# Step sizes of a Mamba-2 mixer with weights loaded instead of tokens, packed in column groups of the array

## The chip, the cores and the metric

The kernel runs on one core of a Trainium2 chip. The metric is the time of one execution on the device in microseconds (us). The median of three runs of the kernel before is 1029.48 us (1029.3 to 1030.61). All data are 32-bit floats, apart from the packed weights of the feed-forward part.

The names of the engines in the profile: PE is TensorE (matmuls), PEld its weight loads, DVE is VectorE, ACT is ScalarE, POOL is GpSimd, SP is SyncE, which here only issues DMAs.

## The reference

The input is 4 sequences of 1024 tokens with 256 features. One layer is applied: `x + norm(mixer(norm(x)))`, then `x + norm(ffn(norm(x)))`. What matters here, cut to its core:

```
zxbcdt = u @ in_proj_kernel            # [.., 256] @ [256, 1288]
z, xBC, dt = 512, 768 and 8 columns of it
xBC = silu(causal_conv1d(xBC))         # x (512), B (128), C (128)
dt  = softplus(dt + dt_bias)           # the step sizes: one per token and head, 8 heads
dA  = dt * -exp(A_log)                 # running sums of dA give all decays of the scan
... chunked state scan with these decays, gate with silu(z), norm, output projection
ffn: gate and up [2048, 256] and down [256, 2048], unpacked from 4-bit codes; gelu(gate) * up
```

The change touches the eight columns of the projection that give `dt`.

## The kernel before

**Segments.** The tokens are cut into nine segments: two of 256 tokens (segments 0 and 1) and seven of 512 (2 to 8). Each goes through a mixer (`mixer(s)`) and a feed-forward part (`ffn(s)`). A segment is worked in chunks of 128 tokens: NC is 2 in the short ones and 4 in the long ones.

**Recorder and planner.** No instruction is issued where it is written. A `Recorder` writes down each one as a step with the tiles that it reads and writes; `issue` then plans all steps on a clock of its own (costs in `weigh`, in ns) and emits them in the planned order. Each engine executes its own list strictly in that order and waits on semaphores. At each moment the planner takes, for an engine, the step with the lowest `rank` among those that could start within a short patience (150 ns in the beginning, 30 ns later); ties go to the earlier recorded. A step's `floor` is the earliest time that the planner may give it. Because all steps go through one helper, every instruction of the profile carries line L347; the tiles' names tell them apart.

**Ranks.** `mix` steps of segment s+2 rank ahead of the matmuls of `ffn(s)`. So the mixer two segments ahead goes first wherever its inputs are there, and the feed-forward matmuls fill the rest of TensorE's time.

**Tiles.** Two PSUM banks of pool `a` serve the mixers from segment 2 on (`ps_a()` hands them out), four of pool `f` and two of pool `d` the feed-forward part. In segment 0 the mixer uses pool `f`, in segment 1 `a` and `d` in turn. A bank is given out in the order in which it was asked for; a later request may pass an earlier one only where two banks are free (`may_start`):

```
if at >= self.ahead or at >= len(self.waiting) or (at > 0 and len(self.free) < 2):
    return None
```

**The mixer's front.** `norm_in` normalises the tokens, turns each chunk with TensorE and copies the result to `xnT`, in two halves of 128 features (kk = 0, 1), each [128 features x 512 tokens]. `step_sizes` multiplies these with the last eight columns of `win` (the projection's weights). In it the tokens are the loaded operand: for each chunk and half, a 128x128 block of `xnT` is loaded and eight columns of `win` are streamed through; the result lies with tokens on partitions. In the profile these matmuls are the group `a<-win,xnT` (and `f<-` and `d<-` in segments 0 and 1). Then VectorE adds the bias (`dtv<-a,dtb`), and a chain of small VectorE operations with one exponential on ScalarE (`dte<-dte`) gives `dt` and `da`. Later `features(f)` makes the 768 columns of xBC (`a<-xnT,win`, four passes of 256 or 512 streamed columns each for a pair of halves), with the convolution on VectorE, and `decays` makes the running sums of `da` (`a<-upper,da`, `a<-da,upper` and so on).

A 32-bit matmul is two rows in the profile: two weight loads and two passes of the moving operand. A transpose is one.

**Feed-forward.** From segment 2 on, each product uses seven sub-products with precomputed weight blocks. These lie in DRAM (`stock`), and `fetch(k)` loads block k (1.8 MB) to one of two halves of `wide`. The first two fetches of segment 2 overwrite the plain gate and up weights, which segments 0 and 1 read; they stand in SP's queue (`wide<-stock`) with the mixer's loads `e<-rows`, `r<-rows`, the input loads `x<-in_u_dram` and the output stores `out_dram<-fo`.

Of the kernel before, what the change touches and what calls it, by code (L numbers as in the profile page):

```python
# [13 lines left out]
ALU = mybir.AluOpType  # L14
PSUM = bass.MemoryType.PSUM

P = 128
EPS = 1e-5
NB, L, DM = 4, 1024, 256
DI, NH, HD, DS = 512, 8, 64, 128  # L20
DPROJ = 2 * DI + 2 * DS + NH
# [9 lines left out]
SWITCH = 1400.0  # L31
WARM, WARM_FROM = 40, 9000.0
EARLY = 150000.0
FRONT = 2 + 1 + NF
MASKED = -1.0e30
MLP = 2048
# [110 lines left out]
class Recorder:  # L147
# [78 lines left out]
    @staticmethod  # L226
    def weigh(st):

        e, n = st.engine, st.n
        if e == "PE":  # L230
            cols = Recorder.width(st.shapes[0])
            if st.name == "transpose":
                return max(109.0, cols * 0.42), 220.0
            if st.shapes[0][0] == 64:
                return 109.0, 220.0
            return 140.0 if cols == 1 else 2 * max(100.0 if cols < 64 else 109.0, cols * 0.837), 220.0
        if e == "DVE":
            if st.name == "bn_stats":
                return 60 + n * 1.05, 130.0
            if st.name == "tensor_scalar" and bass.MemoryType.PSUM not in st.space:  # L240
                return 70 + n * 0.53, 130.0
            return 65 + n * 1.05 + (0 if st.name == "tensor_tensor" else 20), 130.0
        if e == "ACT":
            st.table = {AF.Exp: "exp", AF.Gelu_apprx_tanh: "gelu"}.get(
                st.args[2] if len(st.args) > 2 else None)
            if st.name == "dma_start":
                return 500.0, 0.0
            acc = 93 if "accum_out" in st.kwargs else 0
            return 110 + n * 0.72 + 75 * st.pointers + acc, 160.0
        if e == "POOL":  # L250
            if st.name == "memset":
                return 60 + n * 1.2, 70.0
            if ALU.pow in st.args:
                return 523.0, 70.0
            if st.name == "affine_select":
                return 40 + n * 1.0, 70.0
            return (250 if n < 40 else 60 + n * 1.9), 70.0
        return 60.0, 0.0

    def issue(self, tc, rank, patience):  # L260


# [16 lines left out]
        while len(order) < len(steps):  # L279
# [29 lines left out]
            if e == "ACT" and st.table:  # L309
                table = st.table  # L310
            turn = min(PORT, max(0.0, free["POOL"] - t)) if st.port and t < EARLY else 0.0
            free[e] = t + st.busy + turn
# [50 lines left out]
def rank(st):  # L363
    kind, s = st.key
    if kind == "ffn":
        return 25 + 10 * s if st.engine == "PE" else 5
    if kind == "down":
        return 27 + 10 * s
    return {"load": 0, "small": 11, "mix": 10 + 10 * s if s < 2 else max(21, 10 * s - 10), "w": 14 + 10 * s, "z": 13, "const": 12,
            "warm": 1000, "wu": 11, "x": 5}[kind]  # L370


# [1 line left out]
def mamba_ffn_kernel(  # L374
# [19 lines left out]
    r = Recorder(tc.nc)  # L394
# [4 lines left out]
    def pool(name, shape, k=1, ahead=2, of=None, dtype=F32):  # L399
        of = of or sb  # L400
        return Pool([of.tile(shape, dtype, name=f"{name}{j}") for j in range(k)], ahead)

    def fixed(name, shape):
        return pool(name, shape).get()

    def given(ap):
        return Pool([ap]).get()

    u, w_in, conv_w, conv_b, dt_bias, a_log, d_skip, norm_w, w_out = map(
        given, (u, w_in, conv_w, conv_b, dt_bias, a_log, d_skip, norm_w, w_out))  # L410
    g_pack, g_scale, u_pack, u_scale, d_pack, d_scale, out = map(
        given, (g_pack, g_scale, u_pack, u_scale, d_pack, d_scale, out))
# [5 lines left out]
        "x": pool("x", [P, CMAX, DM], 3), "xnT": pool("xnT", [P, 2, TMAX]),  # L418
        "xc": pool("xc", [P, NF, TMAX]), "xn": pool("xn", [P, DM], 2, 3), "th": pool("th", [P, TMAX], 3, 3),
        "sz": pool("sz", [P, DI // P, TMAX]), "r": pool("r", [P, DI // P, P], 2), "e": pool("e", [P, NH, P], 2),  # L420
        "bt": pool("bt", [P, DS], 2), "xdt": pool("xdt", [P, NH, HD], 2),
        "xw": pool("xw", [P, NH, HD], 2), "y": pool("y", [P, DI // P, P], 3),
        "yo": pool("yo", [P, DI // P, P]), "xf": pool("xf", [P, 2, P], 2),
        "xfT": pool("xfT", [P, 2, TMAX], 2), "act": pool("act", [P, HALF], 3, 3),
# [10 lines left out]
    def get(tag):  # L435
        return pools[tag].get()


    def rows_of(s):
        b, t0, T = SEGS[s]  # L440
        return b * L + t0, T
# [3 lines left out]
    def by_segment(s, tag, cut):  # L445

        if s > 1:
            return cut(get(tag), slice(0, SEGS[s][2]))
        if tag not in shared:
            shared[tag] = get(tag)  # L450
        return cut(shared[tag], slice(SEGS[s][1], SEGS[s][1] + SEGS[s][2]))
# [3 lines left out]
    def load_x(s):  # L455
        r0, T = rows_of(s)
        x = by_segment(s, "x", lambda t, c: t[:, c.start // P : c.stop // P, :])
        r.floor = (0.0, 0.0, 40000.0)[min(s, 2)]
        r.sync.dma_start(out=x, in_=u[r0 : r0 + T, :].rearrange("(i p) d -> p i d", p=P))
        r.floor = 0.0  # L460
        xs[s] = x

    win = fixed("win", [P, 2, DPROJ])

    def load_win(c0, c1, queue=r.sync):
        queue.dma_start(out=win[:, :, c0:c1],
                         in_=w_in[:, c0:c1].rearrange("(k p) m -> p k m", p=P))

    r.key = ("load", 0)
    load_x(0)  # L470
    load_win(2 * DI, DPROJ)
    load_win(DI, 2 * DI)
    small_loads = {}
# [10 lines left out]
    dtb, aneg, cw, cb, dsk, nw = [small_loads[k] for k in ("dtb", "aneg", "cw", "cb", "dsk", "nw")]  # L484
# [3 lines left out]
    ident = fixed("ident", [P, P])  # L488
# [48 lines left out]
    def little(tag, n):  # L537
        return get(tag)[:, :n]
# [118 lines left out]
    def mixer(s):  # L657
# [3 lines left out]
        NC = T // P  # L661
        W = NC * NH
        v_ = {}

        def ps_a():

            v_["n"] = v_.get("n", 0) + 1
            if s == 0:
                return banks_f.get()
            return (banks_d if s == 1 and v_["n"] % 2 else banks_a).get()  # L670
# [17 lines left out]
        def step_sizes():  # L688

            xnT = v_["xnT"]  # L690
            pdt = ps_a()
            for i in range(NC):
                for kk in range(2):
                    r.tensor.matmul(pdt[:, i * NH : (i + 1) * NH],
                                     lhsT=xnT[:, kk, i * P : (i + 1) * P],
                                     rhs=win[:, kk, DPROJ - NH : DPROJ],
                                     start=(kk == 0), stop=(kk == 1))
            v = little("dtv", W)
            r.vector.tensor_tensor(v.rearrange("p (i h) -> p i h", h=NH),
                                    pdt[:, :W].rearrange("p (i h) -> p i h", h=NH),  # L700
                                    dtb.unsqueeze(1).to_broadcast([P, NC, NH]), ALU.add)
            e = little("dte", W)
            r.vector.scalar_tensor_tensor(e, v, -1.0, v, ALU.mult, ALU.max)
            r.scalar.activation(e, e, AF.Exp, scale=-1.0)

            z = little("dtz", W)
            r.vector.tensor_scalar(z, e, 2.0, None, ALU.add)
            r.vector.reciprocal(z, z)
            r.vector.tensor_tensor(z, z, e, ALU.mult)
            z2 = little("dtz2", W)  # L710
            r.vector.tensor_tensor(z2, z, z, ALU.mult)
            r.vector.tensor_scalar(e, z2, 1.0 / 17.0, None, ALU.mult)
            for k in (15, 13, 11, 9, 7, 5, 3):
                r.vector.scalar_tensor_tensor(e, e, 1.0 / k, z2, ALU.add, ALU.mult)
            r.vector.scalar_tensor_tensor(e, e, 1.0, z, ALU.add, ALU.mult)
            r.vector.tensor_scalar(e, e, 2.0, None, ALU.mult)
            dt = v_["dt"] = little("dt", W)
            r.vector.scalar_tensor_tensor(dt, v, 0.0, e, ALU.max, ALU.add)
            da = v_["da"] = little("da", W)
            r.vector.tensor_tensor(da.rearrange("p (i h) -> p i h", h=NH),  # L720
                                    dt.rearrange("p (i h) -> p i h", h=NH),
                                    aneg.unsqueeze(1).to_broadcast([P, NC, NH]), ALU.mult)
# [237 lines left out]
        for j in range(NC + 4):  # L960
            for d, stage in enumerate((inner, scan, gated, way_out, turned)):
                i = j - d
                if 0 <= i < NC:
                    steps.append(lambda stage=stage, i=i: stage(i))
                if d == 0 and j < 2:
                    steps += [lambda c=c: gate(c) for c in (2 * j, 2 * j + 1)]
        assert len(steps) == FRONT + 5 * NC + DI // P
        return steps


    def ffn(s):
        b, t0, T = SEGS[s]
        r0, _ = rows_of(s)
        NC = T // P
# [28 lines left out]
            r.vector.tensor_tensor(at[:, n, :], a, bank[:, T : 2 * T], ALU.mult)  # L1003

        def fetch(k):
            r.sync.dma_start(out=blocks[k % 2], in_=stock[k])

        def token_sums():
            x = xfT[s]
# [93 lines left out]
    mix = [mixer(s) for s in range(ns)]  # L1103

    def do(kind, s, steps):
        for step in steps:
            r.key = (kind, s)
            step()
# [6 lines left out]
    for k in range(WARM):  # L1115
        r.floor = WARM_FROM + k * 220.0
        r.tensor.matmul(idle[:, k % 4 * P : (k % 4 + 1) * P], lhsT=ident, rhs=ident,
                        start=(k == 0), stop=True, skip_group_check=True)
    r.floor = 0.0
    do("mix", 0, mix[0][:FRONT])  # L1120

# [8 lines left out]
    r.floor = 0.0  # L1130
    do("mix", 0, mix[0][FRONT:])
    do("mix", 1, mix[1][:FRONT])
    do("mix", 1, mix[1][FRONT:])
    for s in range(ns):
# [67 lines left out]
```

## Time and profile before

| | us |
|---|---|
| median of three runs | 1029.48 |
| the profiled execution | 1027.49 |
| its span in the profile | 1025.8 |
| PE busy | 1006.5 |
| DVE busy | 637.2 |
| ACT busy | 505.4 |
| matmuls of step sizes, all nine segments (x128) | 16.0 |

The page's busy times are sums over one execution. Matmul rows overlap: a row's length is the latency of one pass, and the distance between the starts of successive rows is what a pass costs TensorE in a stream. The 16.0 us in the last line are the busy time of the three groups (13.2, 1.7 and 1.1 us).

### The profile page before, as it was taken

To read this page: it belongs to the slowest core of one execution; us is meant where nothing else is said; L and a number is where in the kernel's file an instruction comes from. 1 tells how busy PE (TensorE), PEld (TensorE's weight loads), DVE (VectorE), ACT (ScalarE), POOL (GpSimd) and SP (SyncE) were. 2 spreads that over 40 slices of the span, in tenths; PEclk is the share of its full clock that TensorE was granted. 3 is DMA by queue.
4 is the path that set the end of the run, shared out by engine and by line. 5 is a ranking of instruction groups with operands and counts; after the bars stand their busy time and mean duration, and the time that the engine had idled before them with its cause. 6 is when DMAs were issued, how large, how long until landed. Compare 5 with 4: busy or idle time off the path is not lost.

```text
span 1025.8 us, 14550 instructions
## 1 busy us (share of the span) xinstructions
PE 1006.5 (98%) x5174; PEld 808.3 (79%) x5174; DVE 637.2 (62%) x1387; ACT 505.4 (49%) x1224; POOL 291.7 (28%) x475
## 2 busy tenths in 40 slices
PE   7999999989999999999999999999999999999997
PEld 6789877867788668877887778877887788888886
DVE  4896775557665766667676757586568674332431
ACT  4645845427472476336655636466446653332330
POOL 1726643430232113403340235003520145001001
PEclk8999999999999999999999999999999999999999
DMA  7032331414132223113312322231323230242300
GB/s 254 10 102 95 134 114 52 165 31 135 45 150 73 82 101 117 73 55 118 138 73 72 134 77 75 96 119 51 115 98 112 96 134 19 74 144 88 131 19 20
DMA packets 39456, 97.16 MB, mean 95 GB/s; under 512 B 3800, under 2 KB 29896, under 8 KB 35272
## 3 DMA queue, kind: packets, MB, share of 16 engines
q1 hardware_dynamic: 38808, 96.22, 27.3%
q8 instruction: 40, 0.66, 0.3%
q14 instruction: 32, 0.26, 0.1%
q10 hardware_dynamic: 576, 0.02, 0.0%
HBM read 84.58 MB, written 11.66 MB: 94 GB/s over the span
## 4 chain that ended last, share of the span: by engine, by line
PE 94%; DVE 3%; POOL 2%; ACT 1%; DMA 0%; issue 0%; POOLq 0%; ACTq 0%
PE f L347 40%; PE a L347 31%; PE d L347 23%; DVE xc L347 1%; POOL wd L347 1%; DMA aneg<-in_a_log_dram 0%; DVE f L347 0%; POOL rsm L347 0%; POOL rsf L347 0%; ACT act L347 0%; ACT xc L347 0%; DVE fo L347 0%; POOL sz L347 0%; DVE xn L347 0%; DVE wide L347 0%
## 5 line engine op out<-in xcount | busy, mean ns | idle before, releaser
L347 PE MATMUL f<-wide 128*128 128x256 f32 x880 | 256.2, 384 | 0.6 <-DVE f L347 0.3
L347 PE MATMUL d<-wd,big 128*128 128x256 f32 x1024 | 254.1, 380 | 0.0
L347 PE MATMUL f<-xfT,wide 128*128 128x256 f32 (+1 forms) x1024 | 250.3, 355 | 1.0 <-ACT big L347 0.9
L347 PEld LDWEIGHTS d<-wd,big 128*128 128x128 f32 x1024 | 189.7, 190 | 31.0 <-issue 8.3
L347 PEld LDWEIGHTS f<-xfT,wide 128*128 128x128 f32 x1024 | 172.3, 191 | 29.9 <-issue 10.3
L347 PEld LDWEIGHTS f<-wide 128*128 128x128 f32 x880 | 161.6, 191 | 34.3 <-issue 11.8
L347 DVE TENSOR_TENSOR f<-f,sums 128x256 f32<-128x256 f32 x216 | 92.5, 429 | 85.0 <-PE f L347 81.0
L347 PE MATMUL a<-xnT,win 128*128 128x512 f32 (+1 forms) x300 | 136.0, 583 | 0.2 <-DVE xc L347 0.2
L347 DVE SCALAR_TENSOR_TENSOR xc<-a,cw,xc 128x511 f32<-128x511 f32 (+1 forms) x135 | 97.8, 726 | 11.1 <-ACT tail L347 9.0
L347 ACT ACTIVATE big<-f 128x512 f32<-128x512 f32 x108 | 62.5, 597 | 70.2 <-DVE f L347 44.4
L347 DVE TENSOR_TENSOR big<-big,f 128x512 f32<-128x512 f32 x108 | 72.6, 684 | 30.8 <-PE f L347 20.3
L347 PEld LDWEIGHTS a<-xnT,win 128*128 128x128 f32 x300 | 55.3, 190 | 42.9 <-issue 37.5
L347 ACT ACTIVATE e<-e,ncs 128x128 f32<-128x128 f32 x240 | 75.1, 391 | 7.1 <-POOL e L347 6.9
L347 ACT ACT_TABLE_LOAD x56 | 71.8, 1283 | 3.7 <-issue 2.8
L347 ACT COPY f<-f 128x256 f32<-128x256 f32 x104 | 37.5, 361 | 64.2 <-PE f L347 56.4
L347 POOL TENSOR_TENSOR state<-state,dec 128x512 f32<-128x512 f32 x24 | 25.5, 1063 | 143.0 <-PE a L347 124.5
L347 POOL TENSOR_SCALAR rsf<-rsf 128x1 f32<-128x1 f32 x32 | 6.1, 192 | 188.4 <-ACT act L347 187.2
L347 POOL TENSOR_SCALAR_AFFINE_SELECT e<-e 128x1024 f32<-128x1024 f32 x30 | 32.8, 1095 | 92.8 <-DMA e<-rows 92.6
L347 ACT ACTIVATE xc<-a,cb,cw 128x512 f32<-128x512 f32 (+1 forms) x45 | 34.3, 763 | 47.0 <-PE a L347 47.0
L347 PE MATMUL a<-wo,y 128*128 128x256 f32 x232 | 56.1, 383 | 0.5 <-ACT xfT L347 0.5
L347 POOL TENSOR_TENSOR sz<-sz 128x256 f32<-128x256 f32 x64 | 38.6, 603 | 55.1 <-ACT sz L347 53.4
L347 POOL TENSOR_TENSOR y<-xc,dsk 128x512 f32<-128x512 f32 x32 | 33.4, 1059 | 64.7 <-DVE xc L347 43.6
(245 smaller groups left out, 1371.8 us busy)
## 6 DMA issues: line engine op xcount, KB each, us to landing
wide<-stock SPq DMA_DIRECT2D x28, 1792.0 KB, 7.3
e<-rows SPq DMA_DIRECT2D x30, 512.0 KB, 4.2
r<-rows SPq DMA_DIRECT2D x54, 128.0 KB, 4.1
stock<-sums SPq DMA_DIRECT2D x8, 512.0 KB, 2.6
out_dram<-fo SPq DMA_DIRECT2D x32, 128.0 KB, 1.7
x<-in_u_dram SPq DMA_DIRECT2D x7, 512.0 KB, 4.6
stock<-wide SPq DMA_DIRECT2D x6, 512.0 KB, 6.6
win<-in_w_in_dram SPq DMA_DIRECT2D x2, 512.0 KB, 6.8
```

Of the source, the lines that this page charges most:

```text
L347: getattr(getattr(self.nc, st.queue), st.name)(*[real(a) for a in st.args], **{k: real(a) for k, a in st.kwargs.items()})
```

## The change

It has three parts.

1. Step sizes. The eight weight columns get a tile of their own, `dtw`, [128 x 2 x 32]: it is set to zero on POOL and filled by a small DMA ahead of the loads of `win` (columns 8 to 31 stay zero). `dtw` is now the loaded operand (32 columns), and a chunk's 128 tokens are streamed. Chunk i writes partitions 32i to 32i+31 of the bank, that is, column group i of the array; both halves kk accumulate, with the loop over kk outside. ScalarE copies the result to a tile `raw`, one transpose on TensorE turns it back (tokens on partitions) into a second bank of the same pool, and the bias addition reads that, eight of every 32 columns.
2. The planner: a 32-column matmul is weighed at 55 ns; the ranks of the mixers 1, 2 and 3 are 15, 19 and 20 in place of 20, 21 and 21.
3. `fetch(0)` and `fetch(1)` of segment 2 get a floor of 178000 on the planner's clock.

```diff
+FETCH = 178000.0
...
             if st.name == "transpose":
                 return max(109.0, cols * 0.42), 220.0
-            if st.shapes[0][0] == 64:
-                return 109.0, 220.0
+            if st.shapes[0][0] in (32, 64):
+                return 109.0 if st.shapes[0][0] == 64 else 55.0, 220.0
...
-    return {"load": 0, "small": 11, "mix": 10 + 10 * s if s < 2 else max(21, 10 * s - 10), "w": 14 + 10 * s, "z": 13, "const": 12,
+    return {"load": 0, "small": 11, "mix": (10, 15, 19)[s] if s < 3 else 10 * s - 10, "w": 14 + 10 * s, "z": 13, "const": 12,
             "warm": 1000, "wu": 11, "x": 5}[kind]
...
+        "raw": pool("raw", [P, P], 2),
...
     load_x(0)
+    dtw = fixed("dtw", [P, 2, 32])
+    r.gpsimd.memset(dtw, 0.0)
+    r.sync.dma_start(out=dtw[:, :, :NH],
+                     in_=w_in[:, DPROJ - NH :].rearrange("(k p) m -> p k m", p=P))
     load_win(2 * DI, DPROJ)
...
             pdt = ps_a()
-            for i in range(NC):
-                for kk in range(2):
-                    r.tensor.matmul(pdt[:, i * NH : (i + 1) * NH],
-                                     lhsT=xnT[:, kk, i * P : (i + 1) * P],
-                                     rhs=win[:, kk, DPROJ - NH : DPROJ],
-                                     start=(kk == 0), stop=(kk == 1))
+            for kk in range(2):
+                for i in range(NC):
+                    r.tensor.matmul(pdt[i * 32 : (i + 1) * 32, :P], lhsT=dtw[:, kk, :],
+                                     rhs=xnT[:, kk, i * P : (i + 1) * P],
+                                     start=(kk == 0), stop=(kk == 1), skip_group_check=True)
+            raw = get("raw")
+            r.scalar.copy(raw[: NC * 32, :], pdt[: NC * 32, :P])
+            pdt = ps_a()
+            r.tensor.transpose(pdt[:, : NC * 32], raw[: NC * 32, :], ident[: NC * 32, : NC * 32])
+            pdt = pdt[:, : NC * 32].rearrange("p (i h) -> p i h", h=32)[:, :, :NH]
             v = little("dtv", W)
             r.vector.tensor_tensor(v.rearrange("p (i h) -> p i h", h=NH),
-                                    pdt[:, :W].rearrange("p (i h) -> p i h", h=NH),
-                                    dtb.unsqueeze(1).to_broadcast([P, NC, NH]), ALU.add)
+                                    pdt, dtb.unsqueeze(1).to_broadcast([P, NC, NH]), ALU.add)
...
         def fetch(k):
+            r.floor = FETCH if s == 2 and k < 2 else 0.0
             r.sync.dma_start(out=blocks[k % 2], in_=stock[k])
+            r.floor = 0.0
```

More of the change, by code (lines that the diff above doesn't have):

```diff
@@ L420, in mamba_ffn_kernel @@
         "sz": pool("sz", [P, DI // P, TMAX]), "r": pool("r", [P, DI // P, P], 2), "e": pool("e", [P, NH, P], 2),
-        "bt": pool("bt", [P, DS], 2), "xdt": pool("xdt", [P, NH, HD], 2),
+        "bt": pool("bt", [P, DS], 2), "raw": pool("raw", [P, P], 2), "xdt": pool("xdt", [P, NH, HD], 2),
         "xw": pool("xw", [P, NH, HD], 2), "y": pool("y", [P, DI // P, P], 3),
```

## The prediction

> **What bounds the kernel now.** I read the page's busy times and the granted clock of its 40 slices first, then the time by stage, then the timeline around one call of `step_sizes`.
>
> ```profile
> span 1025.8 us, 14550 instructions
> PE 1006.5 (98%) x5174; PEld 808.3 (79%) x5174; DVE 637.2 (62%) x1387; ACT 505.4 (49%) x1224; POOL 291.7 (28%) x475
> ...
> PEclk8999999999999999999999999999999999999999
> ```
>
> ```profile
> 60.00:209.00 149.00, 148.46 (x886) 122.38 (x885) 99.41 (x227) 81.67 (x223) 72.48 (x106) 1.00 0.30 107
> 209.00:219.00 10.00, 5.77 (x26) 3.52 (x25) 5.37 (x16) 2.91 (x11) 4.89 (x13) 0.94 0.26 79
> 219.00:945.00 726.00, 723.79 (x3605) 575.28 (x3604) 461.96 (x987) 370.21 (x859) 184.34 (x298) 1.00 0.27 94
> ```
>
> The columns of these three rows are the stretch, its length, then busy time of PE, PEld, DVE, ACT and POOL. From 60 us on TensorE is never idle but for 4.2 us in 209 to 219, and its granted clock is 1.00. So a pass taken from TensorE between 60 and 209, or after 219, is time gained, unless it only widens a gap. Before 60 us TensorE waits for others, and there a saving is worth nothing by itself.
>
> Now the timeline of one call of the step sizes (segment 8); then of the two kinds of excursions into narrower column groups that the kernel already has, `scan`'s (64 columns, with its first two passes alone) and that of `decays` (32):
>
> ```profile
> 766.64 0.28 PE L347 MATMUL a<-win,xnT 128*128 128x8 f32 x2
> 766.78 1.10 PE L347 MATMUL a<-xnT,win 128*128 128x512 f32 x2
> 767.72 1.62 PE L347 MATMUL a<-win,xnT 128*128 128x8 f32 x14
> 769.20 1.10 PE L347 MATMUL a<-xnT,win 128*128 128x512 f32 x2
> ```
>
> ```profile
> 743.34 0.68 PE L347 MATMUL f<-wide 128*128 128x256 f32 x2
> 743.95 1.09 PE L347 MATMUL a<-e,xdt 128*64 128x128 f32 x16
> 744.98 0.70 PE L347 MATMUL f<-xfT,wide 128*128 128x256 f32 x2
> 745.51 0.38 PE L347 MATMUL f<-wide 128*128 128x256 f32 x1
> ```
>
> ```profile
> 743.95 0.33 PE L347 MATMUL a<-e,xdt 128*64 128x128 f32 x2
> ```
>
> ```profile
> 786.08 0.59 PE L347 MATMUL f<-wide 128*128 128x256 f32 x2
> 786.61 0.41 PE L347 MATMUL a<-upper,da 128*32 128x128 f32 x2
> 786.94 0.70 PE L347 MATMUL d<-wd,big 128*128 128x256 f32 x2
> 787.48 0.38 PE L347 MATMUL f<-wide 128*128 128x256 f32 x1
> ```
>
> Columns: start, length of the group, operation, count. Start to start is what counts. The 14 passes at 767.72 hold TensorE for 1.48 us, 0.11 each, though only eight columns are streamed[...]. The 16 half-width passes at 743.95 take 1.03 us, and their first two lie within 0.33 us where one pass lasts 0.27 to 0.32: they start together, in two column groups.
>
> **What the change removes.** Per long segment 16 passes: 0.14 + 1.48 = 1.62 us in two pieces. The 512-column pass behind each piece starts its successor 0.51 us later (1.10 less its 0.59) where 0.43 is usual, 0.08 twice. Together 1.78 us, times seven. Segment 1 has eight passes, 0.92 us.
>
> **What it adds to TensorE.** 16 passes of 128 columns in groups of 32. At 743.95 a pair costs 0.11 us. With four groups side by side 16 passes are four rounds, 0.44 us. To this comes the change of width. In 743.34 to 745.51 (2.17 us) lie four 256-column passes (0.22 each, and 0.08 after a one-column pass) and eight pairs (0.87): 0.35 is left. In 786.08 to 787.48 (1.40) lie four such passes and two serial ones (0.22): 0.32 is left. I take 0.33 per excursion; the Trainium skill (TensorEngine Tiling (Array Packing), Key Properties) says that changing the tiling mode drains the array, without a figure, and these rows give it. The transpose is one pass more, 0.11 (a full-width pass in the stream). One piece: 0.44 + 0.33 + 0.11 = 0.88, a gain of 0.90. Before, five of the seven long calls were in two pieces (a 128x512 pass between, as at 766.64), since the second half of `xnT` is copied 0.5 us after the first. Now four matmuls wait for each half. `features` can't step between any more: the transpose's bank is ahead of its own in the queue of pool `a`, and two free banks would be needed. Feed-forward passes can. A call in two pieces pays two excursions: 1.21, a gain of 0.57.
>
> **A rule that speaks against it.** TensorE: Matmul & The Clock Gate, Part 3 (The mechanism), states that a weight load overlaps running matmuls only where the row group differs. All of these have the full 128 rows. By the rule 16 loads (0.108 us for 128x32 in the rows of `a<-upper,da`) would stand between 16 passes of 0.107: 3.4 us a call, some 2 us slower than now, or 14 us in all. The rows contradict it: full-row passes at 0.11 have loads of 0.19 beneath them, and the half-width pairs keep 0.11 with two loads of 0.136 each. I follow the rows.
>
> **The sum.** Segments 3 to 8, half of them in one piece: 3 x 0.90 + 3 x 0.57 = 4.4 us. Segment 2 (117 us) runs into the gap at 209, which waits for its own mixer's last chunks: I count 0.4 of 0.57 to 0.90. Segment 1: four rounds 0.44, one to three excursions (two pieces, and a transpose of 64 rows, which no row shows: between 0.11 and 0.44), so 0.88 to 1.54 against 0.92 to 1.0: a loss of 0.2. Segment 0, below: a loss of 0.5. In all -4.1 us.
>
> **Start (segment 0).** VectorE is the engine to watch: it sat idle 2.66 us before `dtv` at 13.26 and then has gaps of only some 5 us until 59, the largest 2.0 at 22.2. `dtv` now also waits for the copy (0.27 us, as `bt<-a`, and its semaphores) and for a transpose that the planner puts behind passes of `features`, which cost about 0.43 each there at the low clock: about 2 us later. The gap at 22.2 (it waits for ScalarE, which has its own order) takes up most. I take +0.5, between -0.3 and +2.5. The new DMA: `dtw` is cleared first on POOL (0.1 to 0.2 us, all constants behind it later by that; the first that TensorE needs comes at 3.0, in filler). With rank 0 and the recorded order its DMA becomes second in SP's queue, so both `win` loads and x of segment 1 go out 0.5 us later, and the loads behind them, each of which waits for a semaphore of an earlier DMA, by up to 2. It is 256 pieces of 32 bytes; `dtb` and `aneg`, 128 such pieces each, landed 3.7 and 4.7 us after issue. So it lands near 6 us, and is needed after 11. The large loads are used at 17 and later. Cost nothing, while that cover of 3 to 5 us stands; without it, up to 2.
>
> **Other queues.** ScalarE: nine copies, 2.4 us of 1025 on an engine busy 49%. VectorE: the same number of instructions (0.19 each for `dtv`). The chain to `da` gets 1 to 2 us longer per segment. In segment 2 it is covered: `dte` waited until 130.75 for ScalarE to load the exponential's table (`dtv` was done at 119.3). In segment 3 it isn't (225.15, then 225.60), and `decays` comes later by that; feed-forward passes fill TensorE then. Behind the waiting transpose stand those same passes, but the planner leaves 600 ns between a ScalarE result and TensorE.
>
> **Ranks and the floor.** No kind has a rank from 15 to 21 but mixers 1, 2 and 3, and these keep their order; a tie was decided by the recorded order, which is the same. So the ranks change nothing. The fetches:
>
> ```profile
> 180.04 0.33 SPq L347 DMA_DIRECT2D e<-rows  x1
> 181.52 1.62 SPq L347 DMA_DIRECT2D wide<-stock  x2
> 211.42 2.28 SPq L347 DMA_DIRECT2D out_dram<-fo  x2
> ```
>
> They can't leave before segment 1's last read of `wide`, and the next item on SP is 28 us on. On the planner's own clock (no time of the chip) the old due times are 170.6 and 171.9, behind the last `e<-rows` (169.3) and ahead of the store at 199.9. The floor of 178 keeps them in the same slot. Nothing, unless the new plan has moved `e<-rows` past 171, in which case it keeps that load from standing behind 1.8 MB.
>
> **Rivals.** (a) Four groups don't run side by side, only two: no row shows four. Then eight rounds, 0.87 us: gains of 0.47 and 0.14, in all 1.8 + 0.1 - 0.7 = 1.2 us: 1028.3. Against it: nothing in the half-width rows hints at a limit; their pairs cost what one full pass costs. (b) Slower: the new plan holds up mixer 2's tail. There the feed-forward work has run out, so each us of delay is a us of gap. The turns of its last chunks follow each other by 3.3 to 4.4 us (205.76, 209.91, 214.27, 217.55). The order of a few hundred steps is dealt anew by a planner that charges 0.44 + 0.11 for what costs 0.88 or 1.21. If one exponent load or one chunk falls behind by two turns, 8 us, the result is -4.1 + 8, 1033.4; it decides from 6.2 us. For it: the gap is there already (4.2 us). Against it: every other stage has cover. (c) The change does nothing for time, the gaps growing by what is saved: 1029.5.
>
> **How the numbers follow.** The profiled execution took 1027.49 us (span 1025.8), 2.0 below the median of 1029.48. The sum puts it at 1023.4; against the median, 1025.4. A measurement of this kernel can tell about 0.2%, 2.1 us, from no change. My forecast (the gain passes through, 2.1 to 6.4 us): 0.58, own range 1023 to 1027.4. Rivals (a) and (c): 0.25. Rival (b): 0.17. All calls in one piece and a smaller gap at 209 would give 1021.5; at the other end two turns lost with part of the gain, 1032.5.
>
> **What would show it.** Right: groups of x16 or 8 + 8 with 128*32 for `dtw`, a call at 0.77 us or two of 0.55 start to start, PE busy 4 us lower and idle time unchanged. Wrong: rounds of 0.22 (rival a), a gap after 209 well over 4 us (rival b), `dtv` of segment 0 past 16 us with the first feed-forward pass later than 60 (the start).

## The result, and the profile after

| | kernel before | changed kernel |
|---|---|---|
| median, us (5 runs each) | 1029.3 (1027.69 to 1030.61) | 1036.45 (1033.95 to 1038.71) |
| profiled execution, us | 1027.49 | 1036.45 |
| its span, us | 1025.8 | 1034.6 |

The ratio is 1.0069, with a 95% interval of 1.0049 to 1.0089: 7 us slower. The forecast was 4 us faster.

First the changed kernel's page: busy times, and the granted clock in 40 slices of 26 us.

```profile
PE 1008.3 (97%) x5183; PEld 798.8 (77%) x5183; DVE 634.5 (61%) x1387; ACT 506.5 (49%) x1231; POOL 291.7 (28%) x476
...
PEclk8999999999999989999999999999999999999999
```

PE busy should have fallen by 4 us. It rose by 1.8, and the 15th slice of the clock shows an 8 where before there was a 9. That slice reaches from 362 to 388 us. The time by stage finds the place (stretch, its length, busy PE, PEld, DVE, ACT, POOL, then granted clock, DMA share, GB/s):

```profile
...
209.00:223.00 14.00, 9.00 (x40) 6.64 (x40) 8.55 (x27) 3.14 (x12) 6.99 (x18) 0.94 0.19 58
...
356.00:376.00 20.00, 15.61 (x45) 8.09 (x44) 13.87 (x23) 12.42 (x30) 4.99 (x6) 0.83 0.23 65
```

From 356 to 376 us TensorE is idle for 4.4 of 20 us, at a granted clock of 0.83, and issues 45 matmul rows. The kernel before issues 81 in the same stretch, is idle for 1.0 us, and has clock 1.00:

```profile
356.00:376.00 20.00, 19.00 (x81) 13.65 (x80) 14.89 (x26) 16.66 (x37) 5.36 (x6) 1.00 0.32 91
```

The gap behind 209 us, where rival (b) of the prediction was placed, grew only from 4.2 to 5.0 us. Three single gaps of 1.4 to 1.7 us are new, at 107, 627 and 760.

The new instructions themselves do what the sum said. Here are the calls of the step sizes in segment 3, in one piece, and in segment 8, in two (start, length of the group, operation, count):

```profile
225.62 0.59 PE L348 MATMUL f<-xfT,wide 128*128 128x256 f32 x2
226.14 0.64 PE L348 MATMUL a<-xnT,dtw 128*32 128x128 f32 x16
226.71 0.70 PE L348 MATMUL f<-wide 128*128 128x256 f32 x2
227.25 1.88 PE L348 MATMUL a<-xnT,win 128*128 128x512 f32 x4
...
771.12 0.81 PE L348 MATMUL f<-wide 128*128 128x256 f32 x3
771.87 0.43 PE L348 MATMUL a<-xnT,dtw 128*32 128x128 f32 x8
772.22 0.70 PE L348 MATMUL f<-xfT,wide 128*128 128x256 f32 x2
772.85 0.43 PE L348 MATMUL a<-xnT,dtw 128*32 128x128 f32 x8
773.21 0.70 PE L348 MATMUL f<-wide 128*128 128x256 f32 x2
773.74 1.88 PE L348 MATMUL a<-xnT,win 128*128 128x512 f32 x4
```

From start to start, eight packed passes take 0.35 us and sixteen 0.57. But the full-width passes beside them are slower too: the two between the pieces take 0.63 us (772.22 to 772.85), where two take 0.43 in a stream. So a call is counted, as in the prediction, over a stretch with its neighbours. From 225.62 to 227.25 (1.63 us) lie four 256-column passes (0.86): 0.77 is left for a call in one piece. From 771.12 to 773.74 (2.62 us) lie seven (1.51): 1.11 is left for a call in two. The prediction had 0.77 and 1.10; with rounds of two, as in its rival (a), a call in one piece would take 1.20. The transpose adds 0.11 (775.46 to 775.57). Segment 3's call alone of the seven long ones is in one piece.

SP's queue keeps its order, with `e<-rows` ahead of the two fetches:

```profile
184.75 0.33 SPq L348 DMA_DIRECT2D e<-rows  x1
185.12 0.91 SPq L348 DMA_DIRECT2D wide<-stock  x2
```

**Where TensorE waits.** The timeline of TensorE in the bad stage; the brackets give the idle time before a group and what ended it:

```profile
362.01 0.70 PE L348 MATMUL f<-wide 128*128 128x256 f32 x2
363.54 0.46 PE L348 MATMUL a<-xc 128*128 128x128 f32 x2 [0.82 <-DVE xc L348]
363.83 0.27 PE L348 MATMUL a<-ident,xc 128*128 128x128 f32 x1
364.89 0.48 PE L348 MATMUL a<-ident,xc 128*128 128x128 f32 x1 [0.79 <-DVE xc L348]
366.02 6.45 PE L348 MATMUL a<-xnT,win 128*128 128x512 f32 x8 [0.65 <-DVE e L348]
372.30 0.60 PE L348 MATMUL a<-ident,xc 128*128 128x128 f32 x4
373.87 0.49 PE L348 MATMUL a<-xc 128*128 128x128 f32 x2 [0.97 <-DVE sz L348]
374.20 0.27 PE L348 MATMUL a<-ident,xc 128*128 128x128 f32 x1
375.06 0.70 PE L348 MATMUL f<-xfT,wide 128*128 128x256 f32 x2 [0.59 <-ACT big L348]
```

The short waits on VectorE's `xc`, `e` and `sz` belong to mixer 4's own steps. What is missing is what fills them elsewhere: from 362.71, where the two passes of 362.01 end, to 375.06 there is no feed-forward pass (`f<-` or `d<-`), for 12.35 us. The longest such stretch of the kernel before, between 335 and 392 us, is 3.4 us. The last bracket says what the next one waited for: the gelu, `big<-f` on ScalarE, which reads the gate products from banks of pool `f`. So ScalarE's order is the thing to read. The changed kernel's:

```profile
360.42 2.43 ACT L348 ACTIVATE e<-e,ncs 128x128 f32<-128x128 f32 x8
...
364.30 2.44 ACT L348 ACTIVATE e<-e,ncs 128x128 f32<-128x128 f32 x8
...
373.12 1.28 ACT L348 ACT_TABLE_LOAD   x1
374.41 1.09 ACT L348 ACTIVATE big<-f 128x512 f32<-128x512 f32 x2
```

And that of the kernel before:

```profile
359.50 1.28 ACT L347 ACT_TABLE_LOAD   x1
360.79 1.09 ACT L347 ACTIVATE big<-f 128x512 f32<-128x512 f32 x2
...
364.59 1.28 ACT L347 ACT_TABLE_LOAD   x1
365.88 3.32 ACT L347 ACTIVATE e<-e,ncs 128x128 f32<-128x128 f32 x11
```

Before, ScalarE switches to the gelu's table, is done with two gate products at 361.9, and then does mixer 4's exponentials. After, the exponentials of two chunks come first, and the gelu starts 13.6 us later. The changed kernel saves two table loads of 1.28 us on an engine that had time (54 in place of 56), and TensorE pays for it. It pays twice: the eight 512-column passes at 366.02 take 6.45 us, and the granted clock from 366 to 376 is 0.72. In the kernel before eight such passes took 3.69:

```profile
353.09 3.69 PE L347 MATMUL a<-xnT,win 128*128 128x512 f32 x8
```

The planner's rule for this switch is in `issue`:

```
for st in other:                 # needs another table than the loaded one
    when[st] += SWITCH           # 1400
if len(other) < len(when):
    same = min(when[st] for st in when if st not in other)
    if same <= now + 300.0:
        for st in other:
            del when[st]
```

On the planner's own clock, which is no time of the chip, the gelus are due at 342.7 and with the charge of 1.4 us at 344.1 in the changed kernel; the exponentials are due at 343.6, so they win by 0.5 us. In the kernel before ScalarE is free at 348.0, the gelu with the charge stands at 349.4, the exponentials at 349.9: the gelu wins by 0.5 us. A shift of 1 us turns the decision.

### The profile page after: what moved, and what is told of

Read it like the earlier page. It is cut to its first block, busy times and chain, and to the rows that moved or that the text cites. A ratio compares the mean times of both kernels' runs of the same rounds, so it can differ in the third digit from the quotient of the medians.

```text
span 1034.6 us, 14598 instructions
## 1 busy us (share of the span) xinstructions
PE 1008.3 (97%) x5183; PEld 798.8 (77%) x5183; DVE 634.5 (61%) x1387; ACT 506.5 (49%) x1231; POOL 291.7 (28%) x476
## 4 chain that ended last, share of the span: by engine, by line
PE 91%; POOL 3%; DVE 3%; ACT 1%; issue 1%; DMA 0%; POOLq 0%; ACTq 0%
PE f L348 39%; PE a L348 29%; PE d L348 23%; DVE xc L348 1%; POOL sums L348 1%; POOL rsm L348 1%; POOL wd L348 0%; POOL sz L348 0%; POOL one L348 0%; DMA aneg<-in_a_log_dram 0%; ACT L348 0%; DVE f L348 0%; POOL rsf L348 0%; POOL y L348 0%; ACT sz L348 0%
## 5 line engine op out<-in xcount | busy, mean ns | idle before, releaser
L348 PE MATMUL a<-xnT,win 128*128 128x512 f32 (+1 forms) x300 | 138.1, 590 | 0.9 <-DVE e L348 0.7
L348 PEld LDWEIGHTS a<-wo,y 128*128 128x128 f32 x232 | 43.6, 190 | 6.9 <-ACT xfT L348 0.7
```

The lines of the kernel that those rows point to most:

```text
L348: getattr(getattr(self.nc, st.queue), st.name)(*[real(a) for a in st.args], **{k: real(a) for k, a in st.kwargs.items()})
```

## The experiments

The theory, after the first reading: the instructions saved what the sum says, and the newly dealt order of the steps costs more than that. Rivals: the new instructions cost more than they seem to; the second bank of pool `a` holds up the mixer; the wrong weight in `weigh` spoils the plan. The reading of ScalarE's order above was made after the first eight runs. The last two runs test it.

### The new instructions in the old order

```diff
+ # planned with the old 16 passes; emitted in their place:
+ for kk in range(2):
+     for i in range(n):
+         matmul(bank[i*32:(i+1)*32, :P], lhsT=dtw[:, kk, :], rhs=xnT[:, kk, i*P:(i+1)*P], ...)
+ scalar.copy(raw, bank)
+ ...   # just ahead of the next pass into this bank:
+ transpose(bank[:, P:P+n], raw, ident)
```

> The changed step sizes (dtw, column groups, copy, transpose), but every engine keeps the order of the kernel before: the eight packed matmuls stand in one piece where the old ones ended, the transpose just before the next pass that needs the bank, in the same bank. Theory A (the instructions are cheaper, the new order loses the time): 0.9 us less per long segment, six to seven of them, 1023 to 1025 us, no gaps near 360, 627 and 760 us. Rival B (the new instructions themselves stall TensorE, by changes of width or by the longer chain to the bias addition): 1030 or more, as slow as the change.

Measured: 1027.18 us (before on the same chip 1028.52), ratio 0.9984 (0.9973 to 0.9994). Its timeline of TensorE, segment 8:

```profile
767.43 0.64 PE L384 MATMUL a<-xnT,dtw 128*32 128x128 f32 x16
768.00 1.12 PE L350 MATMUL a<-xnT,win 128*128 128x512 f32 x2
768.97 0.27 PE L358 MATMUL a<-ident,raw 128*128 128x128 f32 x1
769.52 1.98 PE L350 MATMUL a<-xnT,win 128*128 128x512 f32 x4 [0.28 <-DVE dtv L363]
```

The gaps at 627 and 760 are gone, and from 356 to 376 PE is busy 19.00 us at clock 1.00. So the loss belongs to the order. The gain is 2 to 4 us short of what was expected, and the last line says why: the next pass goes into the bank that `dtv` still reads, and starts 0.44 us late, in all six calls of segments 3 to 8 and once before.

### The old instructions in the new order

```diff
- matmul(pdt[i*32:(i+1)*32, :P], lhsT=dtw[:, kk, :], ...)    # not emitted
- scalar.copy(raw, pdt)                                      # not emitted
- transpose(pdt, raw, ident)
+ for i in range(n):                                         # in the transpose's place
+     for kk in range(2):
+         matmul(bank[:, i*NH:(i+1)*NH], lhsT=xnT[...], rhs=win[:, kk, DPROJ-NH:], ...)
```

> The mirror image: the old step sizes (16 passes with eight streamed columns), put where the changed kernel has its transpose, in the order of the changed kernel on every engine; packed matmuls and the ScalarE copy are gone. Theory A: the gaps near 360, 627 and 760 us stay, and the old passes cost 0.6 us more per long segment: 1036 to 1041 us. Rival B: about 1029, as before the change.

Measured: 1040.63 us, ratio 1.0125 (1.0101 to 1.0148). Its stage:

```profile
356.00:376.00 20.00, 15.46 (x50) 8.51 (x49) 14.89 (x25) 13.26 (x32) 5.40 (x6) 0.91 0.29 89
```

The same hole, with 54 table loads and 11.3 us without a feed-forward pass, and none of the new instructions. The order alone costs 12 us. Within it the new instructions are 4 us cheaper than the old ones (1040.63 against 1036.45).

### One bank

```diff
- pdt = ps_a()
- r.tensor.transpose(pdt[:, : NC*32], ...)
+ r.tensor.transpose(pdt[:, P : P + NC*32], ...)
```

> The change with the transpose written to other columns of the same bank, so that no second bank of pool a is asked for ahead of features; the plan is made anew. Theory A1 (the second bank holds features back, which makes the plan's extra gaps): gaps at 356 to 375 us mostly gone, 1027 to 1031 us. Theory A2 (any new deal of the order loses, whatever the banks): within 3 us of the change, 1033 to 1040.

Measured: 1033.9 us, ratio 1.0045 (1.0028 to 1.0061). The time lies in the range of A2, but the hole is mostly gone, as A1 has it: the gelu comes first here, and the longest stretch without a feed-forward pass is 3.9 us. Instead late starts of 0.4 to 1.3 us are new from 229 to 234, and the one at 214 grew from 2.1 to 2.8. Since everything was planned anew, it can't be told what the bank itself costs.

### The old kernel with one price changed

```diff
+ if cols == NH:
+     return 69.0, 220.0      # one old step-size matmul; was 200
```

> The kernel before with one number changed: the planner is told that an old step-size matmul costs 69 ns (as cheap a call as it takes the new one for) in place of 200. The instructions are those of before, only their order is dealt anew. Theory A2 (any new deal loses): 1032 to 1040. Theory A1 (it is the changed banks and chain that make the gaps): within 3 us of before, 1026 to 1033.

Measured: 1032.78 us, ratio 1.0039 (1.0024 to 1.0054). This lies in both ranges. No instruction differs from the kernel before, and the time is 4 us longer. The new losses lie elsewhere (three of 0.4 to 0.7 us at 77 to 79, one of 2.0 us at 106.7), not at the changeover. So a new deal of the same instructions can cost 4 us; this one run does not show that any would.

### The new instructions in the old order, without the wait

```diff
- if mine & taken or passed > 1800.0:
+ if mine & taken or passed >= 800.0:       # transpose behind one 512-column matmul
+ # steps on the bank held until 900 ns of other TensorE work have been emitted
```

> The changed step sizes in the order of the kernel before, as in the first experiment, but the transpose comes one or two passes earlier and two or three feed-forward passes stand between it and the next matmul into its bank, so that TensorE doesn't wait 0.44 us for the bias addition. Theory A (a call in one piece saves 0.8 to 0.9 us): 7 x 0.44 = 3 us less than the first experiment, about 1024 us. Rival (the wait is only moved, to the copy or to a later pass): 1027 again.

Measured: 1023.43 us (1022.35 to 1026.08), before 1028.08, ratio 0.9956 (0.9942 to 0.997). It beats both kernels. Its timeline:

```profile
764.63 0.64 PE L385 MATMUL a<-xnT,dtw 128*32 128x128 f32 x16
765.21 1.12 PE L350 MATMUL a<-xnT,win 128*128 128x512 f32 x2
766.17 0.27 PE L359 MATMUL a<-ident,raw 128*128 128x128 f32 x1
766.28 0.60 PE L350 MATMUL f<-wide 128*128 128x256 f32 x2
```

The wait behind the transpose is gone, and the gain is 4.6 us, for a sum of 4.1 in the prediction.

### Mixer 4 later

```diff
  def norm_in():
+     r.floor = 320000.0 if s == 4 else 0.0     # planned at 308000 without
```

> The change with one floor more: the mixer of segment 4 may not start before 320 on the planner's clock (308 without it), so that its convolution stage no longer falls on the changeover from the feed-forward part of segment 2 to that of segment 3. Theory P (the loss at 356 to 375 us is this coincidence): that gap and the low clock behind it go, 6 to 10 us less than the change, 1026 to 1031. Rival (a new deal loses anywhere): the gap moves elsewhere, 1033 to 1040.

Measured: 1026.82 us, ratio 0.9982 (0.9972 to 0.9992), 9.6 us less than the changed kernel. Its stage:

```profile
356.00:376.00 20.00, 20.00 (x86) 14.98 (x85) 16.46 (x40) 12.39 (x24) 1.26 (x2) 1.00 0.51 172
```

With mixer 4's chunks moved off the changeover from `ffn` of segment 2 to that of segment 3 the stage is full. That places the loss at the meeting of the two, but leaves open what it is in it that stops TensorE.

### Without the floor on the fetches

```diff
- r.floor = FETCH if s == 2 and k < 2 else 0.0
+ r.floor = 0.0
```

> The change without its floor of 178000: in this plan the first two weight-block loads then stand ahead of two r loads and the last e load of segment 2. If the floor matters as the planner has it, 5 to 8 us slower than the change, 1041 to 1045, with a longer gap after 209. If the prediction was right that it does nothing: 1034 to 1038.

Measured: 1042.35 us, ratio 1.0141 (1.012 to 1.0163), 6 us more than the changed kernel. SP's queue:

```profile
182.12 0.32 SPq L348 DMA_DIRECT2D wide<-stock  x1
182.57 1.69 SPq L348 DMA_DIRECT2D r<-rows  x2
184.36 0.56 SPq L348 DMA_DIRECT2D wide<-stock  x1
186.17 0.32 SPq L348 DMA_DIRECT2D e<-rows  x1
```

One fetch of 1.8 MB has gone ahead of mixer 2's `r<-rows` loads and the other ahead of its last `e<-rows`; in the 30 us from 200 TensorE is busy 20.2 us, in the changed kernel 24.7.

### The true price

```diff
- return 109.0 if st.shapes[0][0] == 64 else 55.0, 220.0
+ return 109.0 if st.shapes[0][0] == 64 else 137.0, 220.0
```

> The change with the planner told 137 ns for a 32-column matmul in place of 55: a call in two pieces at its measured price of about 1.1 us. Theory M (the plan is bad because the price is wrong): 1026 to 1031. Rival (the price isn't it; the gap at the changeover stays): 1032 to 1039.

Measured: 1033.47 us, ratio 1.0038 (1.0026 to 1.005). Less than the changed kernel, but the hole stays (54 table loads, 10.4 us without a feed-forward pass). The price in `weigh` isn't its cause.

### The gelu first

```diff
+ if 342000.0 <= now < 346000.0 and table == "exp":
+     due = [st for st in other if st.key == ("ffn", 3)]
+     when = {st: t for st, t in when.items() if not due or st.table != "exp"}
+     other = []
```

> The changed kernel, with one decision of the planner reversed: at the changeover to the feed-forward part of segment 3, ScalarE takes the two gelus ahead of mixer 4's first exponentials, as it does in the kernel before. In the changed kernel the exponentials came first and both banks of gate products stood full; TensorE had no feed-forward pass from 362.7 to 375.1 us (13 us; before at most 4). Theory (this one choice on ScalarE is what the loss at 356 to 376 hangs on): no stretch over 5 us without a feed-forward pass there, PE busy 19 or more of the 20 us, and 7 us less in all, 1027 to 1031. Rival (VectorE's convolution in that stage is the bound, whatever ScalarE does): gaps stay, at least 3 us lost there, 1033 or more. What the rest of the order does after the choice is dealt anew too: 2 us either way.

Measured: 1029.23 us (before 1028.92), ratio 0.9999 (0.9986 to 1.0011), 7 us less than the changed kernel. ScalarE:

```profile
360.40 1.28 ACT L352 ACT_TABLE_LOAD   x1
361.70 1.08 ACT L352 ACTIVATE big<-f 128x512 f32<-128x512 f32 x2
...
366.16 1.28 ACT L352 ACT_TABLE_LOAD   x1
367.46 4.49 ACT L352 ACTIVATE e<-e,ncs 128x128 f32<-128x128 f32 x15
```

The longest stretch without a feed-forward pass is 3.3 us, and PE is busy 18.64 of the 20 us (19 was expected) at clock 1.00. VectorE has its convolution to do as before (15.3 us busy of the 20, in the changed kernel 13.9), so it is not what bounds the stage. Outside it nothing is won: the late starts of the table below, without those from 345 to 385 us, add up to 16.4 us here and to 16.3 in the changed kernel.

### The exponentials first, in the kernel before

```diff
+ if 346000.0 <= now < 355000.0:
+     when = {st: max(t, 355000.0) if st.table == "gelu" else t for st, t in when.items()}
```

> The kernel before, unchanged in every instruction, with the same decision reversed the other way: the two gelus of segment 3's feed-forward part are held back by the planner until mixer 4's exponentials of the first two chunks are done (two switches of ScalarE's table fewer). Theory: a stretch of 10 to 14 us without a feed-forward pass at about 360 to 375, TensorE's clock lowered behind it, and 6 to 10 us more, 1034 to 1039. Rival (the stage needs the new step sizes, or VectorE is the bound there): within 3 us of the kernel before, 1026 to 1032.

Measured: 1035.64 us, ratio 1.0066 (1.0042 to 1.009), with the instructions of the kernel before and two table loads fewer. TensorE:

```profile
361.45 1.35 PE L349 MATMUL f<-wide 128*128 128x256 f32 x4
...
367.17 5.40 PE L349 MATMUL a<-xnT,win 128*128 128x512 f32 x8 [1.38 <-DVE xw L349]
...
375.16 0.70 PE L349 MATMUL f<-xfT,wide 128*128 128x256 f32 x2 [0.59 <-ACT big L349]
```

The hole is there again: 12.4 us without a feed-forward pass (362.80 to 375.16), the slow eight passes, and the wait for `big` at its end.

All kernels side by side. Table loads are those of the whole execution; the stretch is the longest between 335 and 392 us from the end of one feed-forward pass (`f<-` or `d<-`) to the start of the next, my own reading too; late starts are my own sum from the trace, over 345 to 385 us and over the whole: by how much one matmul starts later behind the last than 0.84 ns per streamed column (0.11 us at least), where that is over 0.3 us.

| kernel | table loads | stretch, us | late starts 345 to 385 | in all |
|---|---|---|---|---|
| before | 56 | 3.4 | 1.1 | 12.1 |
| new in old order | 56 | 3.4 | 1.1 | 16.4 |
| new in old order, no wait | 56 | 4.1 | 1.8 | 13.9 |
| one bank | 56 | 3.9 | 3.3 | 19.4 |
| old with one price changed | 56 | 3.8 | 1.5 | 16.6 |
| mixer 4 later | 68 | 3.3 | 0.0 | 14.6 |
| gelu first | 58 | 3.3 | 1.4 | 17.8 |
| changed kernel | 54 | 12.3 | 8.1 | 24.4 |
| old in new order | 54 | 11.3 | 6.7 | 22.9 |
| without the floor | 54 | 9.6 | 5.4 | 27.0 |
| true price | 54 | 10.4 | 8.2 | 22.3 |
| exponentials first | 54 | 12.4 | 7.4 | 19.6 |

Every kernel with 54 table loads has the hole, and no other has it.

## Why the prediction was wrong

- **The saving was there, of the size counted.** A call in one piece costs 0.77 us and one in two pieces 1.11; with the transpose 0.88 and 1.22, against 1.78 before. Of segments 3 to 8 five calls came in two pieces where three were counted, so that they gain 3.8 us in place of 4.4. In the old order without the wait every call is in one piece: segments 3 to 8 save 5.4 us and segment 2's some 0.4 (its gap was not seen to shrink), 5.8 in all. Late starts grew by 1.8 us there; 4.0 is left, and 4.6 was measured. That this lies near the sum of 4.1 is partly luck: the sum had three calls in two pieces and 0.7 us of losses in segments 0 and 1, and no late starts.
- **The failed step is "every other stage has cover".** The sum had no term for the new order; its only place was rival (b), at mixer 2's tail, with 0.17. The order costs 12 us with the old instructions. 7.0 of the 12.3 us by which the changed kernel's late starts exceed those before lie between 345 and 385 us, and one decision on ScalarE makes them: turned back it takes 7 us off the changed kernel, and put into the kernel before it adds 7 us. So the kind of loss was that of rival (b), a stage that the new plan holds up, but the place and the engine were others; the gap at mixer 2's tail grew by 0.8 us only. The cover there was feed-forward passes, and these need ScalarE's gelu; I read ScalarE as an engine busy 49% whose nine new copies cost nothing, and did not ask what the order of its table switches holds up.
- **The rest of the order.** With the gelu first the changed kernel is still 5.8 us above the same instructions in the old order without the wait. Its late starts are 3.9 us more (17.8 against 13.9), and six second excursions at some 0.33 are 2.0. No run tells apart why those single gaps (106.7, 218, 753 us in that kernel) came with this deal.
- **The floor** was set at nothing "unless the new plan has moved `e<-rows`". In the new plan the fetches without it go ahead of mixer 2's loads, and it is worth 6 us. The exception named was the case.
- **The start** was put at 0.5 us later. `dtv` of segment 0 came at 11.88 us instead of 13.26, two microseconds earlier at its first matmul (9.52 against 11.51) rather than two later. Nothing of that lead is left at segment 1's call, which starts at 60.29 us, before at 59.87. The small DMA was second in SP's queue, as counted, but x of segment 1 went out 2.1 us later (4.36 against 2.29), not 0.5.
- **The ranks** change nothing: with the old ones the planned order of every engine is the same.
- **What would have shown it.** An engine's share of busy time says nothing of whom its order holds up. The profile before shows the gelu at 360.79 between two table loads, just ahead of mixer 4's exponentials; in `issue` that decision falls by 0.5 us on the planner's clock. With a step chain 1 to 2 us longer per segment, as the prediction itself said, it was open which way it would fall.

## What to carry to other kernels

Where a planner deals the order, price a change twice: its instructions in the old order, and the new order with the old instructions. Look for decisions that hang on a fraction of a microsecond, above all the choice of which table ScalarE loads next, and ask which engine's banks stand full meanwhile. An engine that is half idle can stop the busy one by doing things in the cheaper order for itself.

## What the runs showed of the hardware

TensorE's granted clock can fall behind idle pieces of less than a microsecond. In the changed kernel it was 0.50 from 364.8 to 371.6 us; in the 4 us up to its fall TensorE had sat idle for 0.43, 0.82 and nearly 0.79 us:

```profile
364.80:371.60 6.80, 6.06 (x8) 2.67 (x9) 3.05 (x5) 3.58 (x10) 3.04 (x3) 0.50 0.00 0
```

Eight passes of 512 columns took 6.45 us there, not 3.69. In the run with the exponentials first they took 5.40, with a clock of 0.50 from 367.8 to 371.2. I had counted an idle microsecond as one microsecond; in the changed kernel some 2.8 us of slow passes came on top, although the prediction's own row of 209 to 219 has a clock of 0.94.

Such pieces don't always do it. The run without the floor has the same hole with idle pieces of the same length, and its clock was 1.00 from 356 to 376:

```profile
370.89 0.33 PE L348 MATMUL a<-ident,xc 128*128 128x128 f32 x1 [0.79 <-DVE xc L348]
372.02 3.70 PE L348 MATMUL a<-xnT,win 128*128 128x512 f32 x8 [0.80 <-DVE e L348]
```

So the slow passes are a part of the loss that the hole can have or not have. What decides it no run here shows.

Four column groups of 32 run at the same time with 32-bit data: the four passes of a round start 7 ns apart, a round every 0.11 us, and the 16 passes of a call in one piece took 0.57 us from the first start to the next instruction's. With the slower full-width passes ahead of and behind them that is 0.77 us.
